# Third layer's experts: gathered rows in five buffers, asked for three experts ahead

## The chip, the cores and the metric

The kernel runs on one core of a Trainium2 chip, as one launch. The metric is the device time of the launch in microseconds (us). The engines of the core are TensorE (PE in the profile), VectorE (DVE), ScalarE (ACT), GpSimd (POOL) and SyncE (SP). They run side by side, each in its own fixed order of instructions, and wait for each other by semaphores. DMAs are issued from the queues of SP, POOL and ACT.

## The reference

Four layers, each `x = x + s * g`, where `s` is an attention-like part and `g` the SiLU of a feed-forward part, both of the layer-normed `x`. `x` has 2 x 1024 rows of 128, in float32. Only the third layer is touched. Cut to what matters, for its T = 2048 rows:

```python
# s: the "circuits" part
attn_out = quantum_circuit(x.reshape(B, T, H, dk))   # cumprod(cos(v)) over dk = 8
x1 = layer_norm(x + attn_out, gamma1, beta1)
q = quantum_circuit(x1[..., :16])
h = einsum('btq,fq->btf', q, w1) + b1                # 16 -> 512
s = layer_norm(x1 + relu(h) @ w2.T + b2, gamma2, beta2)

# g: 16 experts; each takes the C = 256 rows that score highest for it
scores = softmax(flat_x @ gate_w.T).T
topk_weight, topk_idx = top_k(scores, C)
xg = flat_x[topk_idx]                                # 16 x 256 x 128
h = gelu(xg @ Wg.T) * (xg @ Wu.T)                    # 512 wide
eo = (h @ Wd.T) * topk_weight
out = zeros.at[topk_idx].add(eo)                     # scatter-add
shared = (gelu(x @ Sg.T) * (x @ Su.T)) @ Sd.T
g = silu(out + shared)
```

## The kernel before, in words

The 2048 rows are 16 tiles of 128 (`NT`), taken in four groups of four (`NG`). `l2_layer` (L1403) is the third layer. It opens its SBUF and PSUM pools in a `with`; the order in which pools are opened decides their addresses, so it also decides which tiles of layer two a new tile lies on and has to wait for.

`enter2` layer-norms each group (`enter`, L132: BN statistics and `sh` on DVE, `rs` on POOL at L72, four passes of 128 columns on ACT at L99), writes the rows to a DRAM tensor `rows` and computes gate scores. The scores go to `rows` too (144 columns in all). Then two streams of work are woven together by `weave.run(main, side, n_main, n_side)` (L165): both are Python generators, each `yield` is a step, and before each step of `main` the helper takes steps of `side` as long as `done * n_main < (j + 1) * n_side`. So `n_side / n_main` is the rate of the side work. For PE, DVE and ACT the order in which the code is emitted is the order in which it runs (`manual_schedule`, L1703). POOL and SP are ordered by a scheduler, and in the entry to the layer so are DVE and ACT (only PE is by hand there, L1445).

The first weave has the search for each expert's 256 rows (`chosen.search`) as main work, and beside it the shared expert (`shared`, L1588, whose hidden tile `hs` has a single buffer of its own) and the first steps of the circuits.

The second weave (L1705) has `experts()` (L1639) as main work, 97 steps, and `rest()` beside it: `circuits` (L1461, DVE and ACT: products at L1476, statistics at L83 and L84, layer norm at L97, L99, L109, L111), `last_weights` (L1496: am, a, qsc, qrsc, wq), and `forward` (L1525, mostly PE: transposes q2t, matmuls h2p and y2p, then layer norm of y).

For expert `ex`, in the order of the code:

- `hidden(w, xT, 0, ...)` (L1573): two groups of matmuls, f2g and f2u (L1582), the gelu f2a on ACT (L1584) and the product `h` on DVE (L1586).
- f2y (L1661): the output matmuls of the expert before, `ex - 1`; then `ye` (L1671): its rows times their weights, on DVE.
- two scatters (`scatter`, L1632, two halves of 128 rows): indirect DMAs on POOL that add the rows of `ye` to the DRAM tensor `adds`. Each waits, by `after`, for the two scatters of the expert before, because two experts may hold the same row.
- behind each of these two scatters a gather (`gather`, L1618, indirect DMA on POOL) of rows of expert `ex + 2` into a tile `xg`, of which there are three buffers.
- `turned(ex + 1)` (L1624): two transposes of the next expert's rows (xgt, L1627) and a copy xT on ACT (L1629); then `hidden(w, x, 2, ...)`, the second half of this expert's hidden columns.

Before the first expert, gathers of experts 0, 1 and 2 are issued. The weights `w` (three buffers) and `wd` (two) come by SP's queue. After the last scatter the fourth layer reads `adds` (f2z, L1822).

Of the kernel before, what the change touches and what calls it, by code (L numbers as in the profile page):

```python
# [11 lines left out]
F32 = mybir.dt.float32  # L12
# [7 lines left out]
P = 128  # L20
B, S, D = 2, 1024, 128
# [14 lines left out]
E2, I2, IS2 = 16, 512, 256  # L36
# [117 lines left out]
def after(tc, i, others):  # L154

    for x in others:
        tc.add_manual_dep(
            i.ins,
            x.ins.name,
            mybir.DependencyInfo(mybir.DependencyClass.Sync, mybir.DependencyReason.DATA),  # L160
            reason="rows that indirect transfers wrote",
        )
# [1240 lines left out]
def l2_layer(k):  # L1403

    nc, tc = k.nc, k.tc
    with (
        tc.tile_pool(name="l2", bufs=1) as pool,
        tc.tile_pool(name="l2g", bufs=1) as gp,
        tc.tile_pool(name="l2w", bufs=3) as wp,
        tc.tile_pool(name="l2h", bufs=2) as hp,  # L1410
        tc.tile_pool(name="l2t", bufs=2) as tmp,
        tc.tile_pool(name="l2d", bufs=1, space=bass.MemoryType.DRAM) as dr,
        tc.tile_pool(name="l2p", bufs=4, space=PSUM) as pm,
        tc.tile_pool(name="l2q", bufs=1, space=PSUM) as pq,
# [12 lines left out]
        rows = dr.tile([NT * P, D + E2], F32, tag="rows", name="rows2")  # L1427
# [145 lines left out]
        def hidden(w, xT, j, h, name):  # L1573

            n = xT.shape[1]
            m = 512 // n
            pg = PS.tile([P, m, n], F32, tag="mm", name=f"f2g{name}_{j}")
            pu = PS.tile([P, m, n], F32, tag="mm", name=f"f2u{name}_{j}")
            a = tmp.tile([P, m, n], F32, tag="a", name=f"f2a{name}_{j}", bufs=3)
            for c, ps in ((0, pg), (1, pu)):  # L1580
                for i in range(m):
                    nc.tensor.matmul(ps[:, i, :], lhsT=w[:, c, j + i, :], rhs=xT, start=True, stop=True)  # L1582
                if c == 0:
                    nc.scalar.activation(a, pg, AF.Gelu)  # L1584
                yield
            nc.vector.tensor_tensor(h[:, j : j + m, :], pu, a, ALU.mult)  # L1586

        def shared():  # L1588
            w = k.wm("sh").rearrange("p (a c d) -> p a c d", a=3, d=P)
            nj = IS2 // P  # L1590
            for n in range(NG):
                h = hp.tile([P, nj, 512], F32, tag="hs", name=f"hs{n}", bufs=1)
                for j in range(nj):
                    yield from hidden(w, k.xnT[:, n * 512 : (n + 1) * 512], j, h, f"s{n}")
                py = PS.tile([P, 4, D], F32, tag="y", name=f"f2ys{n}")
                for i in range(4):
                    for j in range(nj):
                        nc.tensor.matmul(
                            py[:, i, :],
                            lhsT=h[:, j, i * P : (i + 1) * P],  # L1600
                            rhs=w[:, 2, j, :],
                            start=(j == 0),
                            stop=(j == nj - 1),
                        )
                    if i == 1:
                        yield
                y = tmp.tile([P, 4, D], F32, tag="a", name=f"ys{n}", bufs=3)
                nc.scalar.copy(y, py)
                nc.sync.dma_start(av[:, 4 * n : 4 * n + 4, :], y)
                yield  # L1610

        def row_of(ex, f):
            return bass.IndirectOffsetOnAxis(ap=chosen.idx[f][:, ex : ex + 1], axis=0)

        xg = {}
        added = k.added = []

        def gather(ex, f):  # L1618
            if ex < E2:
                if f == 0:  # L1620
                    xg[ex] = hp.tile([P, 2, D + E2], F32, tag="xg", name=f"xg{ex}", bufs=3)
                nc.gpsimd.indirect_dma_start(xg[ex][:, f, :], None, rows, row_of(ex, f))

        def turned(ex):  # L1624
            pt = PS.tile([P, 2, P], F32, tag="t", name=f"xgt{ex}")
            for f in range(2):
                nc.tensor.transpose(pt[:, f, :], xg[ex][:, f, 0:D], k.ident)  # L1627
            xT = hp.tile([P, 2 * P], F32, tag="xT", name=f"xT{ex}")
            nc.scalar.copy(xT, pt.rearrange("p f t -> p (f t)"))  # L1629
            return xT  # L1630

        def scatter(ex, f, ye):  # L1632
            i = nc.gpsimd.indirect_dma_start(adds, row_of(ex, f), ye, None, compute_op=ALU.add)
            if f:
                tc.declare_no_dep(i.ins, added[-1].ins, reason="an expert's tokens are different ones")
            after(tc, i, added[2 * (ex - 1) : 2 * ex])
            added.append(i)

        def experts():  # L1639

            nj = I2 // P
            for ex in range(3):
                for f in range(2):
                    gather(ex, f)
            xT = turned(0)
            yield
            last = None
            for ex in range(E2 + 1):
                if ex < E2:
                    w = wp.tile([P, 2, nj, P], F32, tag="w", name=f"w2_{ex}")  # L1650
                    nc.sync.dma_start(w.rearrange("p a c d -> p (a c d)"), k.i["l2_e"][ex][:, 0 : 2 * I2])
                    wd = wp.tile([P, nj, P], F32, tag="wd", name=f"wd2_{ex}", bufs=2)
                    nc.sync.dma_start(wd.rearrange("p c d -> p (c d)"), k.i["l2_e"][ex][:, 2 * I2 :])
                    h = hp.tile([P, nj, 2 * P], F32, tag="h", name=f"h2_{ex}")
                    yield from hidden(w, xT, 0, h, f"{ex}")
                if last is not None:
                    w_, h_ = last
                    py = PS.tile([P, 2, D], F32, tag="cnt", name=f"f2y{ex}")
                    for f in range(2):
                        for j in range(nj):  # L1660
                            nc.tensor.matmul(  # L1661
                                py[:, f, :],
                                lhsT=h_[:, j, f * P : (f + 1) * P],
                                rhs=w_[:, j, :],
                                start=(j == 0),
                                stop=(j == nj - 1),
                            )
                        yield
                    ye = hp.tile([P, 2, D], F32, tag="ye", name=f"ye{ex}", bufs=3)
                    for f in range(2):  # L1670
                        nc.vector.tensor_scalar(  # L1671
                            ye[:, f, :], py[:, f, :], xg[ex - 1][:, f, D + ex - 1 : D + ex], None, ALU.mult
                        )
                    for f in range(2):
                        scatter(ex - 1, f, ye[:, f, :])
                        gather(ex + 2, f)
                if ex < E2:
                    x = xT
                    if ex + 1 < E2:
                        xT = turned(ex + 1)  # L1680
                    yield from hidden(w, x, 2, h, f"{ex}")
                    last = wd, h

        weave = Weave()

        def rest():
            yield from circuits()
            yield from last_weights()
            yield from forward()

        def early():

            sh = shared()
            for j in range(24):
                next(sh, None)
                if j < 21:
                    next(others, None)
                yield
            for _ in sh:
                yield  # L1700

        others = rest()
        with tc.manual_schedule(engines={E.PE, E.DVE, E.Activation}):  # L1703
            weave.run(chosen.search(scores.rearrange("p (c r) e -> p c r e", r=2)), early(), 18, 24)
            weave.run(experts(), others, 1 + 6 * E2, 122)  # L1705

# [264 lines left out]
def recurrent_kernel(ctx: ExitStack, tc, ins, out):  # L1973
# [74 lines left out]
    with tc.tile_pool(name="w0f", bufs=1, side="right") as wp:  # L2048
# [8 lines left out]
        l0_ffn(k, (w12, hw, w3))  # L2057
    l1_layer(k)
    l2_layer(k)
    l3_layer(k, o)  # L2060

# [107 lines left out]
```

## Time and profile before

| | us |
|---|---|
| median of 3 runs | 1902.19 (1899.86 to 1903.78) |
| the profiled execution | 1908.33 |
| its span in the profile | 1906.6 |
| PE, DVE, ACT, POOL busy in the span | 1675.6, 1257.5, 850.9, 561.7 |
| experts' stage: first gather to first read of `adds` | 1377.0 to 1546.3 |
| 32 gathers, median of one on POOL | 0.987 |
| 32 scatters, median of one on POOL | 1.579 |
| PE's waits for gathered rows, whole stage | 17.7, in 9 waits |

How to read it: times inside the profile are microseconds from the start of the span. "Busy" is the time in which an engine runs an instruction; matmuls are pipelined, so two rows of PE may overlap. A DMA on POOL is busy while POOL prepares it, and the data land later. "[3.41 <-DMA xg<-rows,idx]" behind a row says that the engine stood idle for 3.41 us before it, and that the landing of that DMA ended the wait. The granted clock is PE's, 1.00 at full speed. A releaser named in a row is the one that came last by the profile; where it had long been done, it was another.

### The profile page before, as it was taken

What the parts mean: (1) busy time and instruction counts of PE and PEld (TensorE: products, weight loads), DVE (VectorE), ACT (ScalarE), POOL (GpSimd) and SP (SyncE); (2) the same over time, 40 slices, a digit from 0 to 9 for tenths busy, and PEclk for the clock granted to TensorE, in tenths of its full rate; (3) what the DMA queues carried; (4) which work ended last, traced back from release to release, by engine and by line L of the source; (5) the groups of instructions that cost most, each with busy time, mean ns of one, the idle gap of its engine ahead of it and who ended that gap; (6) DMA issues with size and microseconds to landing.
All of it is one profiled execution on the core that took longest, in us unless ns stands there. A gap on an engine that the chain in (4) does not pass through costs nothing.

```text
span 1906.6 us, 24480 instructions
## 1 busy us (share of the span) xinstructions
PE 1675.6 (88%) x7703; PEld 870.1 (46%) x7727; DVE 1257.5 (66%) x2597; ACT 850.9 (45%) x1849; POOL 561.7 (29%) x888
## 2 busy tenths in 40 slices
PE   4999999999999999989997598876579947999996
PEld 2344444444444444433445355544367833444442
DVE  3988888888879888873002464667763447777771
ACT  1555555555555555543213154432133333666564
POOL 2233333333333333331003442220055531112201
PEclk9999999999999999999998699986689978999998
DMA  5333333233424333332000564302044423112100
GB/s 194 97 94 76 93 89 101 72 99 86 103 68 103 84 81 79 88 89 58 0 0 1 128 179 118 76 21 64 17 104 104 100 62 78 31 50 57 38 2 12
DMA packets 114164, 142.88 MB, mean 75 GB/s; under 512 B 28324, under 2 KB 95284, under 8 KB 112292
## 3 DMA queue, kind: packets, MB, share of 16 engines
q1 hardware_dynamic: 87860, 89.13, 18.5%
q0 software_dynamic: 25840, 52.06, 11.0%
q8 instruction: 62, 1.02, 0.2%
q14 instruction: 66, 0.54, 0.1%
q10 hardware_dynamic: 336, 0.13, 0.0%
HBM read 57.53 MB, written 16.19 MB: 39 GB/s over the span
## 4 chain that ended last, share of the span: by engine, by line
PE 52%; DVE 21%; DMA 8%; ACT 6%; POOL 5%; issue 5%; SPq 2%; POOLq 0%; DVEq 0%; ACTq 0%
PE sc L292 10%; PE f0h L450 6%; PE pz L334 5%; DVE nm L302 5%; DMA aT<-tT 4%; PE o3p L699 4%; DVE tT L316 3%; DVE e L312 3%; PE st L1788 2%; PE po L352 2%; ACT e L304 2%; PE pq L268 2%; POOL aT L323 2%; SPq L323 2%; DVE nm L1758 2%
## 5 line engine op out<-in xcount | busy, mean ns | idle before, releaser
L292 PE MATMUL sc<-xnT,q 128*128 128x512 f32 x1024 | 506.3, 596 | 5.9 <-ACT e L304 5.7
L304 ACT ACTIVATE e<-sc,nm 128x1024 f32<-128x1024 f32 x256 | 285.2, 1114 | 342.3 <-DVE nm L302 264.2
L302 DVE TENSOR_REDUCE nm<-sc 128x1 f32<-128x1024 f32 x256 | 307.9, 1205 | 9.1 <-PE sc L292 9.0
L292 PEld LDWEIGHTS sc<-xnT,q 128*128 128x128 f32 x1024 | 194.3, 191 | 234.5 <-issue 189.7
L323 POOL DMA_DIRECT2D aT<-tT x384 | 205.0, 540 | 325.0 <-DVE tT L316 174.2
L334 PE MATMUL pz<-aT,xn 128*128 128x512 f32 x512 | 263.2, 599 | 3.8 <-DMA aT<-tT 3.8
L1797 ACT ACTIVATE e<-st 128x512 f32<-128x512 f32 (+3 forms) x384 | 167.6, 492 | 124.8 <-PE st L1788 99.1
L312 DVE SCALAR_TENSOR_TENSOR e<-e,c,e 128x1024 f32<-128x1024 f32 x128 | 164.1, 1282 | 3.3
L316 DVE STREAM_TRANSPOSE tT<-e 128x1024 f32<-128x1024 f32 x128 | 158.3, 1237 | 1.1 <-DMA aT<-tT 0.3
L334 PEld LDWEIGHTS pz<-aT,xn 128*128 128x128 f32 x512 | 98.2, 192 | 120.1 <-issue 111.5
L72 POOL TENSOR_TENSOR f<-fv,neg_half 128x1 f32<-128x1 f32 x128 | 82.5, 645 | 198.6 <-DVE fv L366 123.8
L1758 DVE TENSOR_REDUCE nm<-sr 128x1 f32<-128x384 f32 (+3 forms) x176 | 105.9, 636 | 36.7 <-PE sr L1750 36.3
L1788 PE MATMUL st<-qs,ks 128*128 128x512 bf16 (+3 forms) x360 | 108.2, 324 | 6.9 <-DMA qs<-nr 4.0
L352 PE MATMUL po<-vc,z 128*128 128x384 f32 x256 | 105.9, 496 | 4.9 <-ACT oc L363 2.2
L450 PE MATMUL f0h<-h,hw 128*128 128x512 f32 x256 | 110.0, 592 | 0.0
L1083 ACT ACTIVATE e<-st 128x384 f32<-128x384 f32 (+1 forms) x128 | 58.6, 477 | 111.8 <-PE st L1047 73.0
L1737 DVE TENSOR_REDUCE nf<-sf 128x1 f32<-128x512 f32 x128 | 82.6, 683 | 19.7 <-PE sf L1736 19.2
L699 PE MATMUL o3p<-e,v 128*32 128x512 f32 (+3 forms) x768 | 87.1, 499 | 0.1
L464 DVE TENSOR_TENSOR f0y<-f0o,bv 128x512 f32<-128x512 f32 x4 | 2.8, 692 | 121.3 <-PE f0o L460 121.3
L352 PEld LDWEIGHTS po<-vc,z 128*128 128x128 f32 x256 | 47.7, 191 | 70.5 <-issue 49.3
L450 PEld LDWEIGHTS f0h<-h,hw 128*128 128x128 f32 x256 | 48.6, 190 | 61.2 <-issue 61.2
L268 PE MATMUL pq<-xnT,m 128*128 128x512 f32 x128 | 69.7, 627 | 6.9 <-ACT oc L363 4.8
(396 smaller groups left out, 2557.7 us busy)
## 6 DMA issues: line engine op xcount, KB each, us to landing
aT<-tT SPq DMA_DIRECT2D x640, 64.0 KB
aT<-tT POOLq DMA_DIRECT2D x384, 64.0 KB
w<-in_l_e SPq DMA_DIRECT2D x16, 512.0 KB
qs<-parts SPq DMA_DIRECT2D x126, 64.0 KB
ks<-parts SPq DMA_DIRECT2D x42, 192.0 KB
parts<-hm SPq DMA_DIRECT2D x14, 384.0 KB
w<-in_l_w POOLq DMA_DIRECT2D x8, 640.0 KB
wd<-in_l_e SPq DMA_DIRECT2D x16, 256.0 KB
```

The source lines that it names most:

```text
L292: nc.tensor.matmul(ps[:, n * 512 : (n + 1) * 512], lhsT=q[:, m, hf * 512 + t * P : hf * 512 + (t + 1) * P], rhs=k.xnT[:, b * S + n * 512 : ...
L302: nc.vector.tensor_reduce(nm, ps, AX.X, ALU.max, negate=True)
L304: nc.scalar.activation(em, ps, AF.Exp, bias=nm, accum_out=(s1, s2)[m][:, t : t + 1])
L312: nc.vector.scalar_tensor_tensor(e[0], e[1], c, e[0], ALU.mult, ALU.add)
L316: nc.vector.transpose(tT[:, :, t % 2, :, :].rearrange("p j J c -> p J j c"), e[0].rearrange("p (J j a) -> p J j a", J=8, j=4),)
L323: (nc.gpsimd if j == 3 or (i == 0 and j > 0) else nc.sync).dma_start(aT[32 * j : 32 * j + 32, t - 1 : t + 1, i, :, :].rearrange("a t J c - ...
L334: nc.tensor.matmul(pz, lhsT=k.xn[:, 8 * b + J, :], rhs=st["aT"][:, :, :, J, :].rearrange("p t i c -> p (t i) c"), start=(J == 0), stop=(J ...
L352: nc.tensor.matmul(po.rearrange("p a d -> p (a d)"), lhsT=st["z"][:, t * P : (t + 1) * P], rhs=mats[h][1].rearrange("p a d -> p (a d)"), s ...
L450: nc.tensor.matmul(ph, lhsT=hw[:, l, c, j * P : (j + 1) * P], rhs=cur[:, c, cols], start=(c == 0), stop=(c == 3))
L699: nc.tensor.matmul(po[32 * i : 32 * i + 32, c0:c1], lhsT=self.v[:, kt, vc : vc + 32], rhs=es[i], start=start, stop=stop, skip_group_check= ...
L1788: nc.tensor.matmul(ps[:, n0:512], lhsT=kk[0:KR, kt // 4, i, kt % 4 * P : (kt % 4 + 1) * P], rhs=q[0:KR, c, i, n0:512], start=not diag, sto ...
L1797: nc.scalar.activation(e[:, n0:512], ps[:, n0:512], AF.Exp)
```

## The change

The gathers of the experts move. Expert `ex + 3` is asked for right behind the first half of expert `ex`'s hidden matmuls, so ahead of the scatters of `ex - 1`, and `xg` has five buffers in place of three. A gather now waits, by `after`, for the second transpose of expert `ex - 3`'s rows (`read`). The room for the two buffers comes from `hs`, which takes the tag `h` of the experts' hidden tile (two buffers, of the same 4 KB per partition). The pool `l2t` (small tiles of layer norms and of `hidden`) is opened first in place of sixth. The rate of the side work is 128 steps for 97 in place of 122.

```diff
     with (
+        tc.tile_pool(name="l2t", bufs=2) as tmp,
         tc.tile_pool(name="l2", bufs=1) as pool,
         tc.tile_pool(name="l2g", bufs=1) as gp,
         tc.tile_pool(name="l2w", bufs=3) as wp,
         tc.tile_pool(name="l2h", bufs=2) as hp,
-        tc.tile_pool(name="l2t", bufs=2) as tmp,
...
             for n in range(NG):
-                h = hp.tile([P, nj, 512], F32, tag="hs", name=f"hs{n}", bufs=1)
+                h = hp.tile([P, nj, 512], F32, tag="h", name=f"hs{n}")
...
-        xg = {}
+        xg, read = {}, {}
         added = k.added = []

         def gather(ex, f):
             if ex < E2:
                 if f == 0:
-                    xg[ex] = hp.tile([P, 2, D + E2], F32, tag="xg", name=f"xg{ex}", bufs=3)
-                nc.gpsimd.indirect_dma_start(xg[ex][:, f, :], None, rows, row_of(ex, f))
+                    xg[ex] = hp.tile([P, 2, D + E2], F32, tag="xg", name=f"xg{ex}", bufs=5)
+                i = nc.gpsimd.indirect_dma_start(xg[ex][:, f, :], None, rows, row_of(ex, f))
+                if ex > 2:
+                    after(tc, i, [read[ex - 3]])
...
             for f in range(2):
-                nc.tensor.transpose(pt[:, f, :], xg[ex][:, f, 0:D], k.ident)
+                read[ex] = nc.tensor.transpose(pt[:, f, :], xg[ex][:, f, 0:D], k.ident)
...
                     yield from hidden(w, xT, 0, h, f"{ex}")
+                    for f in range(2):
+                        gather(ex + 3, f)
...
                     for f in range(2):
                         scatter(ex - 1, f, ye[:, f, :])
-                        gather(ex + 2, f)
...
-            weave.run(experts(), others, 1 + 6 * E2, 122)
+            weave.run(experts(), others, 1 + 6 * E2, 128)
```

On POOL, where the scheduler decides, the built order is: before, after the first six gathers, `rs` twice and then scatter, gather, scatter, gather for each expert, with an `rs` here and there behind such a group. In the changed kernel the first six gathers are followed by four more (experts 3 and 4) ahead of `rs`; then come two scatters of expert `ex` and two gathers of expert `ex + 5` in turn, the `rs` of the layer norms behind a pair or between two gathers. On DVE and ACT the entry into the layer is reordered as well: the BN statistics of the first two groups stand ahead of the last outputs (`ou`, `o`, L657 to L667) of layer two's attention, and four passes of L99 stand ahead of its last copy `oTs` (L685). On SP the first copy into `rows` goes ahead of the first expert's weights.

## The prediction

> **What bounds the kernel now.** I read the page first. Over the whole span TensorE (PE) leads:
>
> ```profile
> PE 1675.6 (88%) x7703; PEld 870.1 (46%) x7727; DVE 1257.5 (66%) x2597; ACT 850.9 (45%) x1849; POOL 561.7 (29%) x888
> ```
>
> That is an average over four layers, and the change touches one stage, so I cut that stage out with the view of busy time by windows. The third layer's experts run from the first gather (1377.0 us after the span's start) to the first read of the finished sums, f2z (1546.3).
>
> ```profile
> 1377.00:1440.00 63.00, 44.66 (x204) 37.19 (x205) 39.14 (x130) 20.73 (x40) 36.18 (x30) 0.81 0.41 95
> 1440.00:1512.00 72.00, 69.98 (x448) 63.76 (x447) 27.59 (x76) 26.23 (x50) 38.35 (x31) 1.00 0.47 111
> 1512.00:1546.30 34.30, 18.39 (x106) 16.25 (x105) 11.40 (x31) 8.27 (x17) 17.90 (x13) 0.85 0.28 40
> ```
>
> Columns: window, length, then busy us of PE, PEld, DVE, ACT, POOL, then the granted PE clock. These are three stages. In the first (experts 0 to 6, beside the "circuits", which are DVE work) nobody is full. In the second PE is full: 69.98 of 72. In the third PE is half idle. So I ask the waits of PE, from 1388 on:
>
> ```profile
> PE xgt L1627 <- DMA xg<-rows,idx: 15.7, 8, 3.4
> PE f2y L1661 <- DVE h L1586: 3.5, 2, 3.1
> PE f2g L1582 <- ACT xT L1629: 1.7, 1, 1.7
> ```
>
> The transposes wait 15.7 us, in 8 pieces, for gathered rows. By the timeline they fall on expert 3 (3.41), 4 (1.74), 5 (0.74+2.42), 6 (0.99+2.79), 11 (1.28), 14 (2.34). A gather is late because on POOL it stands behind a scatter that waits for `ye`. A further 2.02 us, for expert 0's rows, stands before 1388 and stays: POOL issues those six gathers in the same order.
>
> A wait also costs clock. Same windows, PE alone (busy, then clock):
>
> ```profile
> 1405.50:1409.50 4.00, 3.97 (x11) 0.57 0.27 33
> 1414.60:1418.00 3.40, 3.37 (x16) 1.00 0.32 53
> 1434.90:1440.20 5.30, 5.30 (x14) 0.51 0.34 39
> 1515.10:1518.70 3.60, 3.60 (x14) 0.53 0.31 41
> ```
>
> Behind the waits of 3.41, 0.99+2.79 and 2.34 us PE runs at about half clock for 4 to 5 us; behind the 1.74 one (second row) at full. Work lost in the last stretch: 3.6 x 0.47 = 1.7 us; in the third row 5.3 x 0.49 = 2.6; in the first 1.7.
>
> **The change part by part.**
>
> *Gathers three experts ahead, in front of the scatters.* The same 32 gathers (0.99 us each, 0.3 between issues) and 32 scatters (1.58) remain: 2 x 1.88 + 2 x 1.29 = 6.3 us of POOL per expert, against a mean period of (1523.3 - 1388.4)/14 = 9.6 us. POOL has room. Gather k+3 is issued about two periods before its transposes, so the 15.7 us go. The new wait of a gather on transposes `read[k]` is met when it is issued: they precede the matmuls `f2g` of expert k. Five buffers are free two experts earlier than they are needed. Cost of both: 0.
>
> What is late next? In the first stage, DVE. Its order there is fixed, and puts an expert's `h` (0.69) behind a layer-norm step, L109, which waits for four ACT passes (4 x 0.41 = 1.65 us). One row shows what the gather's wait did to that chain:
>
> ```profile
> 1405.12 0.16 DVE L97 SCALAR_TENSOR_TENSOR sh<-mv,rs 128x4 f32<-128x4 f32 x1
> 1409.56 0.69 DVE L109 TENSOR_TENSOR xn<-xn,bv 128x512 f32<-128x512 f32 x1 [4.28 <-ACT xn L99]
> ```
>
> ACT's passes stood behind a gelu `f2a` whose matmul had waited for rows. Without that wait L109 starts 1.8 us after `sh`, at 1407.1: 2.4 us come back on DVE, not 3.4 on PE. PE now waits for h(2) behind L109 and L111: about 1409.0, so f2y of expert 2 starts near 1409.5 instead of 1410.84.
>
> I followed the changed program's order of instructions on each engine on from there with the durations of these rows. Experts 3 and 4: DVE has only 1.8 us of ACT wait per layer norm either way, so nothing more comes back; one `rs` (1.05, POOL), now behind two scatters and a gather, makes DVE wait 1.1 us, against 0.67 before. Expert 6: before, its rows came at 1434.68 and h(5) at 1438.87, after a table load of 1.28 that also waited for PE. Now DVE leaves the q products at 1434.87 - 2.4 = 1432.4, the table is loaded by then, and four small steps (am, a, qsc, qrsc), which the new order puts first, take 2.0: h(5) at 1434.4. That is 4.4 us, and f2y of expert 5 moves from 1441.5 to near 1437.5. Bounds: 2.4 if the matmuls there still run at half clock (two groups of 0.86, so 1.8 more), 6 if DVE issues 6% denser than I count, as it did between 1397.5 and 1405.1 (7.64 us for 8.14 of instructions).
>
> *The second stage* is full of PE work. Only the 1.28 comes back. Transposes that share one PSUM buffer with the q2T copies cost some 0.8 us more than before, since two of them now follow each other. I take +0.5, bounds -0.5 and +1.3.
>
> *Rate 128 for 122.* 5% more steps of the side work per expert's step. The last `y2p` matmuls come behind f2y of expert 11 instead of 12: 8 instructions, 1.78 us, leave the third stage and enter the second. That costs nothing in all; it lets PE end alone.
>
> *The third stage.* From the end of f2y(12) (1511.8) to f2z 34.5 us pass. Out go the wait of 2.34, its half clock of 1.7 and the 1.78 moved forward. What sets the end is the chain of scatters, for each pair waits until the pair before has landed:
>
> ```profile
> 1527.34 1.61 POOL L1633 DMA_INDIRECT adds<-ye,idx  x1 [0.21 <-DVE sh L97]
> 1529.26 1.90 POOL L1633 DMA_INDIRECT adds<-ye,idx  x1 [0.30 <-issue]
> 1535.03 1.54 POOL L1633 DMA_INDIRECT adds<-ye,idx  x1 [3.87 <-DVE h L1586]
> 1536.87 1.54 POOL L1633 DMA_INDIRECT adds<-ye,idx  x1 [0.30 <-DVE ye L1671]
> 1540.85 1.54 POOL L1633 DMA_INDIRECT adds<-ye,idx  x1 [2.44 <-DMA adds<-ye,idx]
> 1542.70 1.54 POOL L1633 DMA_INDIRECT adds<-ye,idx  x1 [0.30 <-issue]
> ```
>
> From a pair's second issue to the next pair: 5.77, 3.98, and 3.63 to f2z. (The third line's "DVE h" had long been done; it waited for the landing.) The chain starts at ye(13). In the new order ye(13) stands behind the last layer norm: f2y(12) ends at 0; ye(12) 1.9; ve 4.4; rs, behind the two scatters of expert 12, 5.7 to 6.7; sh 6.8; four passes to 8.6; L109, L111, h(14), ye(13) done at 11.2. Then 0.1, 1.85, 4.0, 1.85, 4.0, 1.85, 3.63: f2z at 28.5. Gain 34.5 - 28.5 = 6.0, of which 1.8 is only the moved y2p. Bounds: 2 (landings of 5.77 each time: 3.6 more) and 8 (landings of 3.63, and rs not behind the scatters).
>
> *l2t opened first, hs in the tag h.* These move addresses, not work. `h` for hs has no reader to wait for (DVE's order over the search is unchanged). But other addresses mean other waits, and the entry to the layer is reordered: eight BN steps now run before the last `o` of layer two, 1.2 us of DVE, and four ACT passes (1.65) before its copy oTs; while rs (at 1283.23, 1.2 us after its ve, behind the fourth w1 DMA) may go in front of two of those DMAs. The copy of the last projection, which enters the late groups, was at 1286.15, held by the wait for rs; I find 1286.0. Bounds: 1.2 sooner (rs no longer held) and 2.3 later (sh still at 1284.30, then the passes, oTs, yp, copy: 1288.4). I take 0.2.
>
> Sum, in work: 4.4 + 0.5 + (6.0 - 1.8) + 0.2 = 9.3 us. The profiled execution is 1908.33 us, 1.7 outside its span of 1906.6; it would be 1899.0. It lies 6.1 above the median of the runs, 1902.19, so the median becomes **1892.9 us**.
>
> The Trainium skill, page "TensorE: Matmul & The Clock Gate", section "What's actually happening", says that the clock halves after an idle window of about 3.4 us. The trace shows halves behind waits of 2.34 us, so a shorter gap is enough here. By the page those stretches would not come from the waits and would stay.
>
> **The rivals.**
>
> *All of PE's wait comes back* (PE alone bounds): 15.7 us, 1886.5; with 7 us of half clock, 1879. For it: DVE is busy only 39 of 63 us. Against: DVE's idle there is waiting for ACT in a fixed order. 0.13.
>
> *The half-clock stretches stay*: 9.3 - 1.7 - 1.8 = 5.8, so 1896.4. For it: in the first stage PE keeps gaps of 2 to 3 us, now for `h`. Against: the full clock behind 1.74. 0.08. (This is the skill's rule above.)
>
> *Little moves*: the waits turn into waits for `h`, and the landings at the end are long ones. 2.4 + 0 + 0.2 - 1 = 1.6: 1900.6. The same if gathers are still late on POOL, which speaks least, by its 6.3 of 9.6 us. 0.12.
>
> *Slower*: rs now queues behind a whole pair of scatters and of gathers. If this closes into a ring (ye, 3.8 of scatters, 2.6 of gathers, rs 1.05, sh 0.15, ACT 1.65, L109 and L111 1.4, h 0.7, next ye 0.6: 12 us) at each of the eight layer norms, each costs 12 - 9.6 = 2.4 us, 19.2 in all, of which 2.4 (rs in the first stage and before f2z) stands in the sum already: 1892.9 + 16.8 = 1909.7. The gain is gone from four of eight on, and six of eight make it slower. Against: `sh` uses the rs of the group before, save twice. 0.10.
>
> **The numbers.** Forecast 1892.9 (its own range 1889 to 1897): 0.57. Faster by over 0.2% (3.8 us, about what a measurement of this kernel can tell from no change): 0.57 + 0.13 + 0.08 = 0.78; within 0.2%: 0.12; slower: 0.10. The range from 1885.0 to 1901.0 leaves out the slower case and about half of the fastest.
>
> **What would show it.** PE's waits for gathered rows behind 1388: from 15.7 to under 1. PE's f2y waiting for h: from 3.5 to about 10. DVE's longest L109 wait: from 4.28 to about 2. f2y(5) near 1437, f2z near 1537. Clock at 1.00 behind f2y(12). Wrong would be: transposes still waiting for DMA; DVE's sh waiting for rs by more than 2 us more than twice; f2z less than 4 us earlier, with the last pairs still 5 us apart; or the entry later than 1287.

## The result, and the profile after

The changed kernel takes 1886.56 us, the median of 4 runs (1884.14 to 1887.79). The kernel before, run on the same chip, takes 1901.03 us (4 runs, 1899.04 to 1903.78). The ratio of the runs is 0.9919, with a 95% interval of 0.9906 to 0.9932. The medians lie 14.5 us apart; the forecast was 9.3 less.

The two profiled executions lie 24.2 us apart (1908.33 and 1884.14), because unchanged work ahead of the third layer differs from run to run too: from the gate maximum gmx of layer two to the memset of w1, which starts the third layer's entry, 219.2 us pass in the one and 211.8 in the other, and 212.6 to 219.3 in the executions below. So every time below is counted from that memset on.

The three stages of the experts, by the view of windows of the changed kernel (window, length, busy us of PE, PEld, DVE, ACT, POOL, then the granted clock). Its first gather is at 1367.2 and f2z at 1523.2:

```profile
1367.20:1427.40 60.20, 45.16 (x232) 37.83 (x232) 41.45 (x138) 21.75 (x43) 40.15 (x34) 0.89 0.48 113
1427.40:1499.20 71.80, 71.03 (x456) 65.54 (x454) 30.47 (x84) 28.31 (x54) 40.33 (x31) 1.00 0.47 108
1499.20:1523.20 24.00, 11.53 (x70) 9.76 (x70) 6.20 (x15) 3.61 (x9) 11.57 (x8) 0.85 0.29 33
```

The last stage has shrunk from 34.3 to 24.0 us, the first from 63.0 to 60.2, and the clock of the first is 0.89 where it was 0.81. The waits of PE behind the first expert:

```profile
PE f2y L1665 <- DVE h L1586: 6.8, 5, 3.1
PE f2g L1582 <- ACT xT L1631: 2.6, 3, 1.8
PE amT L1504 <- DVE am L1502: 1.6, 1, 1.6
```

No transpose waits for gathered rows any more: 15.7 us have become 0, the wait for `h` has grown from 3.5 to 6.8, and 1.6 for `am` is new. These rows and the three of the prediction are the longest of each kernel; their sum fell from 20.9 to 11.0 us. DVE's waits, in the view for 1380 to 1440:

```profile
DVE xn L109 <- ACT xn L99: 5.8, 4, 1.7
DVE sh L97 <- POOL rs L72: 1.2, 1, 1.2
```

The longest wait of L109 is 1.7 where it was 4.28. At the end, GpSimd's timeline shows the chain of scatters, now in one rhythm:

```profile
1505.92 1.59 POOL L1635 DMA_INDIRECT adds<-ye,idx  x1 [4.48 <-DVE ye L1675]
1507.81 1.55 POOL L1635 DMA_INDIRECT adds<-ye,idx  x1 [0.30 <-issue]
1511.88 1.55 POOL L1635 DMA_INDIRECT adds<-ye,idx  x1 [2.52 <-DMA adds<-ye,idx]
1513.73 1.54 POOL L1635 DMA_INDIRECT adds<-ye,idx  x1 [0.30 <-issue]
1517.67 1.55 POOL L1635 DMA_INDIRECT adds<-ye,idx  x1 [2.40 <-DMA adds<-ye,idx]
1519.52 1.55 POOL L1635 DMA_INDIRECT adds<-ye,idx  x1 [0.30 <-issue]
```

From each pair's second issue to the next pair 4.07, 3.94 and (to f2z) 3.70 us pass. The 5.77 of before is gone.

### The profile page after: what moved, and what is told of

It reads as the page before. It is cut to its first block, busy times and chain, and to the rows that moved or that the text cites. A ratio compares the mean times of both kernels' runs of the same rounds, so it can differ in the third digit from the quotient of the medians.

```text
span 1882.3 us, 24474 instructions
## 1 busy us (share of the span) xinstructions
PE 1670.9 (89%) x7703; PEld 866.5 (46%) x7727; DVE 1256.9 (67%) x2597; ACT 851.2 (45%) x1849; POOL 562.6 (30%) x888
## 4 chain that ended last, share of the span: by engine, by line
PE 53%; DVE 21%; DMA 7%; issue 6%; ACT 6%; POOL 4%; SPq 2%; DVEq 0%; POOLq 0%; ACTq 0%
PE sc L292 12%; PE pz L334 6%; PE f0h L450 6%; DVE nm L302 5%; PE o3p L699 4%; DMA aT<-tT 4%; DVE tT L316 3%; PE st L1791 3%; DVE e L312 3%; PE po L352 2%; SPq L323 2%; ACT e L304 2%; PE pq L268 2%; DVE nm L1761 2%; PE sf L1739 1%
## 5 line engine op out<-in xcount | busy, mean ns | idle before, releaser
L312 DVE SCALAR_TENSOR_TENSOR e<-e,c,e 128x1024 f32<-128x1024 f32 x128 | 164.1, 1282 | 3.3
```

Source lines behind the costliest of these rows:

```text
L312: nc.vector.scalar_tensor_tensor(e[0], e[1], c, e[0], ALU.mult, ALU.add)
```

## The experiments

I held this theory: the gathers' lead removes PE's waits and the half clock behind them; DVE's order takes part back; the chain of scatters sets the end. The rivals: the gain belongs to the rate, or to the pools, or to the place in front of the scatters. One table of all executions, in us; "entry" is from the w1 memset to the third layer's gmx, "search" from there to the first gather (G), "experts" from G to f2z, "rest" from f2z to the end. ye(12) is DVE's `ye` of expert 12, counted from G. Ratios are of all runs of a kernel against those of the kernel before on the same chip; the quotient of the two medians differs from them by up to 0.001 (it is 0.9924 for the changed kernel).

| kernel | entry | search | experts | ye(12) | rest | ratio and interval |
|---|---|---|---|---|---|---|
| before | 24.8 | 75.9 | 169.3 | 134.8 | 360.3 | 1 |
| changed | 22.4 | 77.3 | 156.0 | 128.7 | 359.1 | 0.9919 [0.9906, 0.9932] |
| rate_alone | 24.8 | 75.8 | 172.5 | 141.4 | 360.8 | 1.0022 [1.0006, 1.0038] |
| place_alone | 22.4 | 75.6 | 159.0 | 131.4 | 359.1 | 0.9917 [0.9897, 0.9938] |
| lead_alone | 22.4 | 76.1 | 157.9 | 130.5 | 360.7 | 0.9912 [0.9892, 0.9931] |
| l2t_sixth | 29.4 | 77.3 | 156.1 | 128.6 | 359.4 | 0.9957 [0.9943, 0.9972] |
| l2t_alone | 22.4 | 77.3 | 169.9 | 135.2 | 360.0 | 0.9987 [0.9974, 0.9999] |
| rate_122 | 22.4 | 76.0 | 156.3 | 126.9 | 362.2 | 0.9926 [0.9906, 0.9946] |
| rate_140 | 22.4 | 76.0 | 170.1 | 145.6 | 362.1 | 0.9995 [0.9981, 1.0009] |
| norm_apart | 22.4 | 75.7 | 158.2 | 130.8 | 359.1 | 0.9922 [0.9909, 0.9935] |
| root_first | 22.4 | 75.7 | 155.2 | 127.1 | 359.9 | 0.9920 [0.9901, 0.9939] |
| root_first_140 | 22.4 | 75.7 | 164.1 | 139.8 | 359.4 | 0.9965 [0.9950, 0.9980] |
| two_sums | 22.4 | 75.7 | 156.6 | 131.4 | 364.5 | 0.9928 [0.9909, 0.9946] |
| rate_110 | 22.4 | 75.9 | 152.8 | 122.7 | 360.8 | 0.9907 [0.9894, 0.9921] |

The entry repeats to 0.1 us. The other columns move by 1 to 3 us between executions of the same order, so smaller differences there are not read by themselves.

What made the experts' stage shorter can be read from four rows. It stays at 156.1 us with l2t back in its place and at 156.3 with the rate back, and it is 172.5 with the rate alone and 169.9 with l2t alone. So the gain of 13.3 us there belongs to the gathers. The new tag of `hs` was not run alone.

Part of the movement is PE's clock. Half clock comes back where PE waits for no gathered rows. Three stretches of place_alone, PE alone (busy, then clock):

```profile
1391.80:1396.10 4.30, 4.30 (x18) 0.60 0.45 75
1412.50:1416.40 3.90, 3.90 (x16) 0.56 0.38 105
1426.60:1433.60 7.00, 6.64 (x26) 0.51 0.28 39
```

Work lost there, as busy time times the missing clock: 1.7, 1.7 and 3.2 us, together 6.7. Summed the same way from 15 us behind G to f2z, the kernel before lost 7.5 us, the changed kernel, l2t_sixth and root_first 1.7 each, two_sums 4.9, lead_alone 5.1 and place_alone 6.7. The experts' stage of the kernels with 1.7 takes 155.2 to 156.1 us, that of lead_alone and place_alone 157.9 and 159.0. What decides where a stretch falls was not found.

### The rate alone, the place alone, the lead alone

The kernel before with the rate alone:

```diff
-            weave.run(experts(), others, 1 + 6 * E2, 122)
+            weave.run(experts(), others, 1 + 6 * E2, 128)
```

> The kernel before with rate 128 for 122 and nothing else. Theory (the gathers' lead gave the gain): PE still waits some 15 us for gathered rows behind the first expert; a y2p group (1.78 us) leaves the tail, but most of it goes to PE's waits in front of it. 0 to 3 us faster than before, f2y(12) to f2z 31 to 34.5. Rival (the side work's earlier end gave most of the gain): 6 us or more faster than before, f2y(12) to f2z near 28.7.

It is slower, by 0.22%, and the experts' stage is 3.1 us longer. The expectation of 0 to 3 us less was wrong. Waits of PE:

```profile
PE xgt L1627 <- DMA xg<-rows,idx: 19.5, 9, 3.4
```

The tail did get shorter (from ye(12) to f2z 31.1 us, where it was 34.5), but PE's waits for rows grew from 17.7 to 19.5 (both from 1380 on) and ye(12) came 6.6 later, of which 1.8 is the y2p work moved in front of it. So while rows are late, more side work per step cost more than it gave; how the rest of the 6.6 arises was not followed. The rival falls: the rate gave none of the gain.

The changed kernel with gathers two ahead, in front of the scatters, in four buffers:

```diff
...
-                    for f in range(2):
-                        gather(ex + 3, f)
+                    if ex:
+                        for f in range(2):
+                            gather(ex + 2, f)
```

> The changed kernel, but each expert's rows are asked for only two experts ahead, in front of the scatters, in four buffers. Theory (any lead that lands the rows before their transposes is enough): the gather stands one pair of scatters earlier on GpSimd than before, so its rows are some 10 us early; PE waits for no rows, and the time is that of the changed kernel within 2 us. Rival (three experts are needed): PE waits for rows again, 5 us or more in all, and the kernel is 4 us or more slower than the changed one.

And three ahead in five buffers, but behind the scatters:

```diff
-                    for f in range(2):
-                        gather(ex + 3, f)
...
                     for f in range(2):
                         scatter(ex - 1, f, ye[:, f, :])
+                if ex < E2:
+                    for f in range(2):
+                        gather(ex + 3, f)
```

> The changed kernel, with gathers three experts ahead in five buffers but behind the scatters of the step, as they stood before. Theory (any sufficient lead): rows land a period early, the time is that of the changed kernel within 2 us. Rival (the place in front of the scatters matters, because scatters hold GpSimd's queue): waits for rows of 4 us or more come back and the kernel is 4 us or more slower than the changed one.

Both have the changed kernel's ratio, 0.9917 and 0.9912. The view of PE's waits from 1380 on names no gathered rows in either; this is the top of it for the gathers behind the scatters:

```profile
PE f2y L1663 <- DVE h L1586: 6.6, 5, 3.1
PE f2g L1582 <- ACT xT L1631: 2.8, 2, 2.4
```

Either half of the edit is enough alone. The third expert and the fifth buffer buy nothing more. The experts' stage is 3.0 and 1.9 us longer than in the changed kernel's execution, with 5.0 and 3.4 us more of PE's work lost at half clock; the last section shows that an execution of the same order can differ by as much.

### The pools' order

The changed kernel with l2t in its old, sixth place, and the kernel before with l2t first:

```diff
     with (
-        tc.tile_pool(name="l2t", bufs=2) as tmp,
         tc.tile_pool(name="l2", bufs=1) as pool,
...
         tc.tile_pool(name="l2h", bufs=2) as hp,
+        tc.tile_pool(name="l2t", bufs=2) as tmp,
```

> The changed kernel with the pool l2t opened in its old place. Theory (opening it first moved the layer's entry 2.2 us forward): gmx, counted from the w1 memset, 2 to 2.5 us later than in the changed kernel, and the time 1.5 to 2.5 us above it. Rival (the entry's gain was one run's chance, or is given back in the search): the time within 1 us of the changed kernel.

> The kernel before with the pool l2t opened first and nothing else. Theory (the pool's place, by itself, lets a reciprocal root go in front of two weight transfers on GpSimd): from the w1 memset to gmx 22.4 us for 24.8, time 2 to 3 us (0.12%) below before. Rival (the order is only needed because five buffers move l2t's addresses): 24.8 as before, time within 1 us.

Before with l2t first: the entry is 2.4 us shorter, and the ratio says 0.13%, 2.5 us. The interval only just excludes no change, but the entry takes 22.4 us in every execution with l2t first and 24.8 in both with it sixth and three buffers. So the gain belongs to the pool. GpSimd's timeline of that kernel:

```profile
1268.95 1.80 POOL L1453 MEMSET w<- 128x2048 f32 x1 [20.57 <-PE st L1038]
1270.70 0.53 POOL L1458 MEMSET q<- 128x512 f32 x1
1271.16 0.60 POOL L1455 DMA_DIRECT2D w<-in_l_w  x1
1271.94 1.02 POOL L72 TENSOR_TENSOR rs<-ve,neg_half 128x4 f32<-128x4 f32 x1 [0.18 <-DVE mv L84]
1272.94 1.05 POOL L1455 DMA_DIRECT2D w<-in_l_w  x2
```

The first `rs` starts 3.0 us behind the memset's start; before it was 6.8 (1276.39 to 1283.23). The last projection's copy L690, held by it, comes 7.6 us behind the memset for 9.8.

With five buffers and l2t sixth, the entry is 7.1 us longer than in the changed kernel, not the 2.2 that I expected, and the ratio rises by 0.0038, about 7 us. DVE's rows of this kernel:

```profile
1278.90 0.69 DVE L690 COPY s<-yp 128x512 f32<-128x512 f32 x1 [1.63 <-PE yp L688]
1285.04 0.16 DVE L97 SCALAR_TENSOR_TENSOR sh<-mv,rs 128x4 f32<-128x4 f32 x1 [0.81 <-POOL rs L72]
1301.13 0.42 DVE L1156 TENSOR_REDUCE gmx<-gl 128x16 f32<-128x256 f32 x1 [9.70 <-PE gl L1440]
```

All four groups' statistics now stand behind L690, so the first `sh` comes 6.1 us behind it; in the changed kernel it comes before it (1271.59, L690 at 1275.15). From L690 to gmx 22.2 us pass, where all others have 14.8 to 15.0. The buffers ahead of l2t moved its tiles, and the scheduler of the entry then put the statistics behind the copy. That the new addresses belong to tiles of layer two still in use is how I read it; no row names it. So the pool's new place is worth 7.1 us beside the new buffers: 4.7 of them repair a loss on the kernel before (29.4 for 24.8), and 2.4 are gained.

### Where the side work ends

The changed kernel with rates 122, 140 and 110 in place of 128:

```diff
-            weave.run(experts(), others, 1 + 6 * E2, 128)
+            weave.run(experts(), others, 1 + 6 * E2, 110)
```

> The changed kernel with the side work's rate back at 122. Theory (with rows early, rate 128 only moves side work forward; it pays at the end, where ye(13) stands behind the last layer norm): from the first gather to f2z 157 to 160 us for 156.0, time 1 to 4 us above the changed kernel. Rival (rate 128 costs what it cost alone, 3.1 us): 153 us, time 3 us below the changed kernel.

> The changed kernel with the side work's rate at 140. Theory (the scatters' chain sets the end and starts at ye(13), which waits 4 us behind the last layer norm in DVE's order): the last layer norm moves in front, ye(13) comes right after its matmuls, f2z 2 to 4 us earlier, from the first gather to f2z 152 to 154 us. Rival (more side work per step makes PE wait for h in the first stage, as rate 128 did alone): 157 us or more.

> The changed kernel with the side work's rate at 110, so that the work beside ends with the last expert instead of two experts sooner: the last y2p matmuls stand beside expert 15, and the last layer norm's apply passes behind ye(15), where PE, DVE and ACT are idle while the scatters land. Theory (experts alone run at 5.4 us each, but a pair of scatters takes 5.9 to land, so each expert left alone at the end is paid by the chain; and a lower rate spreads the side work of the first stage, which is short of DVE and not of PE, over more experts): from the first gather to f2z 149 to 153 us for 156.0, f2z to the end unchanged within 1 us, time 3 to 6 us below the changed kernel. Rival (where the side work ends does not matter, only its sum; or the last layer norm now stands in the way of ye(15)): within 2 us of it, or slower.

At 122 the experts take 156.3 us for 156.0, and the intervals of the ratios overlap: with rows early, 122 and 128 are the same. Both expectations of the stage missed. ye(12) comes 1.8 us sooner than at 128 and from there to f2z 2.0 more pass, which is about the 1.78 us of y2p work that stands behind it again; so the prediction's "costs nothing in all" holds.

At 140 all of the gain is gone. I had expected 2 to 4 us less and got 14.1 more. PE, DVE and GpSimd where the last layer norm falls, three views of that kernel:

```profile
1514.97 2.93 PE L1665 MATMUL f2y<-wd,h 128*128 128x128 f32 x12 [7.07 <-DVE h L1586]
```

```profile
1511.74 0.16 DVE L97 SCALAR_TENSOR_TENSOR sh<-mv,rs 128x4 f32<-128x4 f32 x1 [3.52 <-POOL rs L72]
1513.62 0.69 DVE L109 TENSOR_TENSOR s<-s,bv 128x512 f32<-128x512 f32 x1 [1.72 <-ACT s L99]
1514.23 0.68 DVE L1586 TENSOR_TENSOR h<-f2u,f2a 128x512 f32<-128x512 f32 x1
```

```profile
1507.15 1.61 POOL L1635 DMA_INDIRECT adds<-ye,idx  x1 [2.52 <-DVE ye L1675]
1509.07 1.56 POOL L1635 DMA_INDIRECT adds<-ye,idx  x1 [0.30 <-issue]
1510.10 1.61 POOL L72 TENSOR_TENSOR rs<-ve,neg_half 128x4 f32<-128x4 f32 x1
```

`ve` was ready at 1508.2, but `rs` stood behind a pair of scatters; `sh` waited for `rs`, `h` stood behind `sh` and L109, and PE waited 7.07 us and then ran slowly (the f2y takes 2.93 us, where the same twelve matmuls take 1.60 in the changed kernel). This is the slower rival of the prediction, at one layer norm.

At 110 the experts take 152.8 us, inside what I expected, but not where I expected it. ye(12) comes 6.0 us sooner. 20 of the code's y2p matmuls (4.5 us; the profile has two records for each) were moved behind it, so 1.5 us were gained in the first two stages, and the tail, 30.1 us for 27.4, is 1.8 shorter than those 27.4 and 4.5 would make it; both are within what one order moves by. From f2z to the end 1.7 us more pass, where I expected no more than 1. The ratio, 0.9907, is the lowest of all, but 0.0012 (2.3 us) below that of the changed kernel, short of the 3 to 6 us expected, and the intervals overlap. So it is not shown to be slower, and it is faster only by the one profile.

### DVE's order

One step more between a layer norm's ACT passes and L109, at rate 136 so that the eight more steps cost no pace:

```diff
     if gamma is not None:
-        yield
+        yield from range(1 + scalar)
         nc.vector.tensor_tensor(dst, dst, gamma[:, None, :].to_broadcast([P, 4, D]), ALU.mult)
...
```

> The changed kernel with one more step between a layer norm's four ACT passes and DVE's L109, so that an expert's h or ye may stand between them, and rate 136 so that the eight added steps cost no pace. Theory (what is left of PE's waits in the first stage comes from DVE's fixed order, h behind an L109 that waits for ACT): L109's wait falls from 5.8 us to under 4, f2y's wait for h from 6.8 to under 4, time 2 to 4 us below the changed kernel. Rival (ACT and DVE are dependent chains there, whatever their order): within 1 us of it.

The time is the rival's: the ratio is that of the changed kernel within 0.0003. L109's wait fell to 4.5 us, not under 4, and DVE's wait for `rs` rose from 3.1 to 3.8. PE's wait for `h` fell from 6.8 to 1.3 us, but others took its place, in the view of PE's waits (the rows of expert 0 left out):

```profile
PE f2g L1582 <- ACT xT L1631: 6.7, 4, 3.1
PE amT L1504 <- DVE am L1502: 2.2, 1, 2.2
PE f2y L1665 <- DVE h L1586: 1.3, 2, 0.9
```

`xT` is a copy on ACT, behind the four passes. As I read it, the chain through ACT and DVE bounds the first stage, and which of its links PE meets is a matter of order. So "DVE's fixed order takes part back", as I had it, is too narrow. The rate moved with the edit, and what each did was not taken apart.

### The root in front of the scatters

A step's scatters are emitted at its end and bound behind the last `rs`, at rate 128 and at 140:

```diff
...
-            after(tc, i, added[2 * (ex - 1) : 2 * ex])
+            after(tc, i, added[2 * (ex - 1) : 2 * ex] + [k.root])
...
-                    for f in range(2):
-                        scatter(ex - 1, f, ye[:, f, :])
                 if ex < E2:
...
                     yield from hidden(w, x, 2, h, f"{ex}")
+                if last is not None:
+                    for f in range(2):
+                        scatter(ex - 1, f, ye[:, f, :])
+                if ex < E2:
                     last = wd, h
```

> The changed kernel with GpSimd's order altered: a step's two scatters are put at the end of the step and bound behind the last reciprocal root rs, so that rs of a layer norm stands in front of them. Theory (at the end, sh waits 1.9 us for an rs behind two scatters, and ye(13), which starts the chain, comes behind it): DVE's wait for rs falls from 3.1 us to 1.5 or less, f2z 1.5 to 2.5 us sooner, from the first gather to f2z 153.5 to 155 us. Rival (the scatters, now behind rs, start later by as much): 156 us or more.

> The same edit at rate 140. Theory (at rate 140 the last layer norm's rs fell behind a pair of scatters, sh waited 3.5 us, h stood behind L109 and PE waited 7.1 us): PE's longest wait for h falls to 4 us or less, and from the first gather to f2z 165 to 168 us for 170.1. What is left above 156 belongs to PE's waits in the first stage, where eight layer norms and experts are now interleaved otherwise. Rival (the wait is the order of L109 and h, rs or not): 170 us.

At 140 the experts take 164.1 us for 170.1 (I expected 165 to 168), PE's longest wait for `h` is 4.70 for 7.07 (4 or less), and the ratio falls from 0.9995 to 0.9965. So `rs` behind scatters cost about 6 of the 14 us; the rest lies in the first two stages (ye(12) at 139.8 for 128.7), and its cause was not taken apart further. At 128 DVE's wait for `rs` falls from 3.1 to 0.6 us, as expected, and the experts take 155.2 us, between theory and rival, but the ratio is that of the changed kernel. GpSimd's rows tell why the end does not follow:

```profile
1498.61 1.04 POOL L72 TENSOR_TENSOR rs<-ve,neg_half 128x4 f32<-128x4 f32 x1 [6.25 <-DVE ve L87]
1499.94 1.61 POOL L1635 DMA_INDIRECT adds<-ye,idx  x1 [0.29 <-POOL rs L72]
1501.86 1.82 POOL L1635 DMA_INDIRECT adds<-ye,idx  x1 [0.30 <-issue]
1506.17 1.53 POOL L1635 DMA_INDIRECT adds<-ye,idx  x1 [2.49 <-DMA adds<-ye,idx]
```

ye(13) starts at 1503.5, by G 2.8 us sooner than in the changed kernel, but its pair (the last row) goes out only 0.8 sooner: the pair of 12 now goes out behind `rs`, and the pair of 13 waits for its landing. The chain begins one expert earlier.

### The chain of landings

Expert 14's rows are added into a second tensor, zero at the start, so that the pair of 15 waits for 13 only; DVE adds the two sums before each gate:

```diff
-            i = nc.gpsimd.indirect_dma_start(adds, row_of(ex, f), ye, None, compute_op=ALU.add)
+            to = k.adds_b if ex == E2 - 2 else adds
+            i = nc.gpsimd.indirect_dma_start(to, row_of(ex, f), ye, None, compute_op=ALU.add)
...
+            nc.vector.tensor_tensor(z[g], z[g], zb[g], ALU.add)
...
+                fetch_b(g)
+            for g in range(NG):
                 fetch(g)
...
```

> The changed kernel with the rows of expert 14 added into a second tensor in DRAM, set to zero at the start, and the two sums added on DVE before the gate, so that the pair of expert 15 waits for the pair of 13 and no longer for 14. Theory (the chain of landings sets the end): the last pair is issued when ye(15) is ready, 4 us sooner, f2z 4 to 5 us sooner; the added loads and the DVE add in front of each gate (0.7 us) give 1 to 1.5 us back: 2.5 to 4 us below the changed kernel. Rival (something else ends the stage, or the second read of 1 MB costs what it saves): within 1 us of it, or slower.

In time the rival was right: the second read and the add cost more than the chain's wait saved. GpSimd's rows, SP's loads of the two sums, and SP's wait in front of them:

```profile
1509.65 1.59 POOL L1636 DMA_INDIRECT adds<-ye,idx  x1 [4.48 <-DVE ye L1677]
1511.55 1.55 POOL L1636 DMA_INDIRECT adds<-ye,idx  x1 [0.30 <-issue]
1513.41 1.55 POOL L1636 DMA_INDIRECT adds2b<-ye,idx  x1 [0.30 <-issue]
1515.26 1.54 POOL L1636 DMA_INDIRECT adds2b<-ye,idx  x1 [0.30 <-issue]
1517.11 1.55 POOL L1636 DMA_INDIRECT adds<-ye,idx  x1 [0.30 <-DVE bq L540]
1518.96 1.55 POOL L1636 DMA_INDIRECT adds<-ye,idx  x1 [0.30 <-issue]
```

```profile
1522.74 2.03 SPq L1832 DMA_DIRECT2D f2zb<-adds2b  x4
1524.81 3.37 SPq L1828 DMA_DIRECT2D f2z<-adds  x4
```

```profile
SPq L1832 <- DMA adds<-ye,idx: 17.1, 1, 17.1
```

Nothing waits for a landing between the pairs now. f2z starts 15.2 us behind the first of these issues, where the chained kernel takes 17.3. But that is not the landing: the four loads of the second sum (`f2zb`) stand in front of f2z on SP and take 2.07 us to issue. They start at 1522.74, and the row names a scatter into `adds` as what ended SP's wait, 3.78 us behind the last issue, where the chained kernel has 3.70. So by that row the reads begin 13.1 us behind the first issue (154.5 behind G, where the table's 156.6 counts to f2z), and the waits between the pairs are worth 4.2 us, as the theory had it. The last pair had landed by the start of f2z at the latest, so they are worth 2.1 at the least. From the first read to the end 366.6 us pass for 359.1: the two sets of loads, and the adds that wait for both, give 7.5 us back, not 1 to 1.5. So the chain of landings sets the end of the stage, and this way around it costs more than it saves. The ratio, 0.9928, lies 0.0009 above that of the changed kernel, with overlapping intervals. ye(13) came 2.7 us later than in the changed kernel, by the clock that the last section shows.

## Why the prediction was right, and where its sizes were off

The time lies in the range from 1885.0 to 1901.0, though below the forecast's own 1889 to 1897. The mechanism was the predicted one in the main: rows early, DVE and ACT next, the chain of landings at the end. The gain was forecast 5.2 us too small. In work, predicted and measured in the two profiled executions:

| step | predicted | measured |
|---|---|---|
| first stage, to the start of f2y(5) | 4.4 (2.4 to 6) | 7.0 |
| second stage, with the moved y2p counted as work | 0.5 (-0.5 to 1.3) | 2.3 |
| third stage, the same way | 4.2 | 4.0 |
| entry | 0.2 (1.2 sooner to 2.3 later) | 2.4 sooner |
| search | 0 | 1.4 longer |
| sum | 9.3 | 14.3 |

From f2z to the end 1.2 us less pass, within what executions of one order move by.

*The rows' waits go, at no cost on POOL or in buffers*: right. One new wait on transposes was not met when the gather was issued: the first gather of expert 4 stood 2.18 us for a transpose of expert 1 (at 1379.32), where nothing waited for POOL. *The lead of three* was not needed, which the prediction did not ask.

*The first stage* failed at "experts 3 and 4: nothing more comes back". The second L109 came 2.35 us sooner by G (2.4 predicted), but the third came 3.0 sooner and the end of the q products 4.0: L109 had waited 2.07 and not 1.7 there, and small waits of DVE went too, 0.25 for f2u, 0.69 in front of the first q copy and 0.34 for rows. h(5) then came 6.3 sooner, not 4.4. I had followed the long waits only. PE's wait for `h` is 6.8 us, not the 10 expected. h(5) comes 6.2 to 6.6 us sooner in place_alone, lead_alone, l2t_sixth and two_sums as well, so this part is the change. What follows it is partly the clock: ye(5) comes 6.8 us sooner in the changed kernel, but 4.1 in two_sums and place_alone, and the start of f2y(5) comes 5.1 to 7.0 sooner. So part of the 7.0 is luck.

*The half clock* was followed too loosely. The prediction named three stretches behind the waits for rows. The profile before has a fourth, behind the wait of 0.74 and 2.42 us for expert 5 (PE alone):

```profile
1423.60:1427.00 3.40, 3.34 (x10) 0.58 0.00 0
```

That is 1.4 us more than its 6.0; summed in steps of 0.5 us, 7.5 were lost in all. And the link from the waits to the half clock is not shown: place_alone, without a wait for rows behind expert 0, lost 6.7 us, and its stage is still 10.3 us shorter than before. So some 3 of the 13.3 us gained there may go with where the half clock fell in this execution. Only the last stretch, in the third stage, is gone in every execution of the gathers' order at rate 128.

*The second stage*: 1.28 was the wait for rows of expert 11, as predicted. The other 1.0 us is not pinned; the 0.8 us for the shared PSUM buffer was an estimate that no run tested.

*The third stage*: from the end of f2y(12) to f2z 28.7 us, predicted 28.5. The clock is 1.00 behind f2y(12), as predicted.

*The entry* was the largest miss for its size. I had `rs` in front of two of the transfers as a possibility, with a bound of 1.2 us sooner, and it came true at 2.4. The order of the instructions is fixed before a run, so it could have been read as settled. The *search* was 77.3 us in three executions and 75.6 to 76.1 in the others, among them rate_122, rate_140 and rate_110, which have the changed kernel's code up to the gathers; so it is not read as a cost of the change.

*The rivals.* The time is that of "all of PE's wait comes back" (1886.5), but not its mechanism: only 9.9 of 20.9 us of PE's long waits went, and 6.8 for `h` are left. That the times agree is luck. "The half-clock stretches stay" was wrong for this execution (1.7 us are left: 1399.2 to 1405.2, 5.73 us busy at 0.72), but nearly right for place_alone's, whose stage is 3.0 us longer; the rival's price was 3.5. "Little moves" was wrong. "Slower" does not occur at rate 128 (`sh` waits 1.2 and 1.9 us for `rs`); at 140 one such wait (3.52 us) occurs, and the gain is gone. In that rival's sum four of eight layer norms take 4 x 2.4 - 2.4 = 7.2 of the 9.3 us, so the gain is gone from five on.

## What to carry to other kernels

Where a DMA is issued from an engine's queue behind an instruction that waits for compute, try to move it past that instruction, or to give it one more period: here either was enough, so test both before paying for buffers. When work is woven by a rate, measure several rates after each change: 128 for 122 cost 3.1 us with late rows and nothing with early ones, and 140 put a small root behind a pair of scatters, which cost about 6 of the 14 us lost there. Before a stage's length is put down to a wait, look at what else stands in the same queue: f2z came 2.07 us late behind other loads, which looked like a slow landing. A larger buffer moves every pool opened after it, so look at the entry of the layer as well as at the loop.

## What the runs showed of the hardware that I had not expected

The stretches at half clock do not follow from the length of a wait. The changed kernel and two_sums run the same order here, and PE waits the same 1.55 us for `am`. First the changed kernel, then two_sums:

```profile
1421.42 0.27 PE L1504 MATMUL amT<-ident,am 128*1 128x128 f32 x1 [1.55 <-DVE am L1502]
1423.34 1.03 PE L1582 MATMUL f2u<-xT,w 128*128 128x256 f32 x4
1424.71 1.16 PE L1665 MATMUL f2y<-wd,h 128*128 128x128 f32 x8
```

```profile
1422.20 0.27 PE L1504 MATMUL amT<-ident,am 128*1 128x128 f32 x1 [1.55 <-DVE am L1502]
1424.12 1.75 PE L1582 MATMUL f2u<-xT,w 128*128 128x256 f32 x4
1426.52 2.08 PE L1667 MATMUL f2y<-wd,h 128*128 128x128 f32 x8
```

Eight matmuls of f2y take 1.16 us in the one and 2.08 in the other. The granted clock is 1.00 from 1422.7 to 1428.0 in the one and 0.54 from 1423.7 to 1431.0 in the other. ye(5) comes 60.4 and 63.1 us behind G: 2.7 us for nothing that the code does. The Trainium skill, page "TensorE: Matmul & The Clock Gate", section "What's actually happening", says that the activity window runs freely and so the moment of the change varies from run to run. The two executions agree with that. The same section's idle window of some 3.4 us is longer than the wait seen here.

Scatters that add, issued 1.9 us apart without any wait between them, took 13.1 us for six up to the first read of a sum, against 17.3 when each pair waited for the one before. By the releaser that the profile names, the last of them landed 3.78 us behind its issue, and in the chain 3.70: issued close together, they did not land later.
